# A macaron transformer block on one core: a planner with one clock per engine, and TensorE work beside attention in bursts

## The chip, the core and the metric

The kernel runs on one core of a Trainium2 chip. The core has a matrix engine (TensorE, "PE" in the profile, with its weight loads as "PEld"), three engines for elementwise work (VectorE "DVE", ScalarE "ACT", GpSimd "POOL"), and SyncE ("SP"), which here only issues transfers (DMAs). The engines run their own instruction streams in order and wait for each other by semaphores. The metric is the device time of one execution in microseconds (us), the median of several runs; lower is better.

## The reference

`x` is 2 x 1024 x 512 in float32 (2 sequences of 1024 tokens). The block is

```python
x = x + 0.5 * ffn(layernorm(x))
x = x + attn(layernorm(x))
x = x + 0.5 * ffn(layernorm(x))

def ffn(x):                       # base layer plus two of eight low-rank experts
    probs = softmax(xf @ W_router.T)                      # 8 experts
    topk_p, topk_i = top_k(probs, 2);  topk_p /= topk_p.sum()
    w = sum(one_hot(topk_i) * topk_p)                     # (tokens, 8)
    h = einsum('td,erd->ter', xf, lora_A)                 # rank 16
    return x @ W_base.T + b_base + 2.0 * einsum('ter,eor,te->to', h, lora_B, w)

def bitnet_linear(x, weight, scale_param):
    s = maximum(mean(abs(weight), axis=1), 1e-8)
    y = (x @ sign(weight / s).T) * (s * scale_param)
    return nan_to_num(y, nan=0, posinf=1e6, neginf=-1e6)

def attn(x):                      # q: 32 heads of 16; k, v: 8 heads of 16, each for 4 query heads
    q, k, v = bitnet_linear(x, ...) three times
    attn = softmax(q @ k.T / 4)   # over all 1024 keys, no mask
    return bitnet_linear(attn @ v, o_weight, o_scale)
```

`W_base` is 512 x 512, and all products are to be as exact as float32 makes them: the kernel splits q, k and the inputs of the binarised layers into a high and a low part.

## The kernel before

**Tiles.** Tokens lie in tiles of 128, four tiles to a group, two groups to a sequence: (b, g) = (0,0), (0,1), (1,0), (1,1). `first(b, g)` is what a group does before attention: layer norm (`ln_T`: statistics on DVE, power on POOL, normalised tile on DVE or ACT, transpose on PE, copy on ACT), the first feed-forward (`ffn_tiles`), a second layer norm, and the q, k and v projections (`qkv_part`). `second` is what follows attention: `normalize` (division by the softmax sum), `o_proj`, the second feed-forward. `final` and `last` do the same for the last group, (1,1). `ffn_tiles` has a low-rank and router part (`low`, L359, tiles `phf` or `phs`), the choice of experts on DVE, a transpose (`hwp`, L462), and per tile four base matmuls and one of the experts (L384 and L389, `pbf` or `pbs`; f stands for the first feed-forward, s for the second). `binarize` makes the signs of one weight matrix. `finite` is nan_to_num.

**Attention.** There are 32 units (b, query block of 512, key-value head), in that order of nesting. Each unit has 4 turns. Per unit, 32 `m` tiles (L789: 64 rows, the heads 0 and 2 on the lower and 1 and 3 on the upper half of the rows; 128 queries against 512 keys) give the scores of which DVE takes the row maxima (L797, 128 x 512 each). `m_gather` (L802) and `m_place` join the maxima, transpose them on PE (`mp`, L809), split them on DVE and send them by two DMAs from SP into `mq` (L815). Then 32 `e` tiles (128 keys against 512 queries) are made of two matmuls each: the score (L824) and the subtraction of the maxima (L828, `two_r` times `mq`); ACT takes the exponential (L831) into one of 14 buffers `es`. `a_part` multiplies four exponentials by the values in four column strips, in two halves of 256 queries (L862), into the PSUM bank `av`. `unit_end` copies `av` (L840) and stores it to memory (L843); `place` loads a unit's q and k (L738, L746), `place_v` builds its values.

The turns are software-pipelined: in turn n the kernel issues the `m` tiles of turn n, the `e` tiles of turn n - 5 (LEAD) and the products of turn n - 6. The order within a turn is a string, `TURN` (`LEAD_IN` where there is neither `e` nor `A`). In it `m0(3)` is the m tile 3, `e0(2)` and `e1(2)` the two matmuls of e tile 2, `A0` to `A3` the four products. `F` is a place where one slice of other TensorE work may go, `S` the place of `m_place`, and `V`, `W`, `C`, `D` places where DVE or ACT may take one operation of other work. `m_max` and the exponential are recorded right after their matmul.

**The planner.** All of the program is recorded under a manual schedule: the order in which the kernel records instructions is the order on each engine, and this order comes from a small planner. A piece of work is a generator, a `Strand` with a rank (lower goes first); it yields what it needs next: an engine (P, v, a, g, d for PE, DVE, ACT, POOL and SP's DMAs), the engine its input comes from and since when, and how many PSUM banks it takes. It can also wait for resources (`r`), for conditions (`u`), or for other strands (`j`). `Flow` has one integer clock `t`. A strand may go when `t` has reached the end of its last step plus a delay from the table `LATER` (by pair of engines; one table for attention, one, with shorter delays, for what lies before and after). `offer(kind)` lets one strand record one operation, and then the engine is taken for `LASTS` ticks. `play` goes through the five engines at each tick. A tick stands for 0.115 us (`usec`). During attention a turn is worth `BRIEF` = 50 ticks and each slice given 7 more.

PSUM has eight banks: `ps_a` holds `av`, and the pool `ps` has seven for all else. `stock["fb"]` lets other work hold six before attention and two during it.

**The lead-in** starts with `first(0,0)`, `first(0,1)`, `binarize` for k, q, v and o, and `begin`, which places unit 0 and issues its first 16 m tiles. The loop runs until `begin` is done, plus 3 us, and then `attention` takes over. `first(1,0)`, `first(1,1)`, `second` of three groups and `final` are `chains`, started in attention at given turns, at most three at a time. `last` runs at the end. In batch 0 the writes of q to memory are issued on ACT's queue (high part, L573) and POOL's (low part, L580), other writes of q and k on SP's (L584).

Of the kernel before, what the change touches and what calls it, by code (L numbers as in the profile page):

```python
# [15 lines left out]
P = 128  # L16
# [16 lines left out]
def macaron_kernel(ctx: ExitStack, tc: tile.TileContext, x_in, wbT, b_base, wrT, aT, bT,  # L33
# [68 lines left out]
    for e in range(E):  # L102
# [16 lines left out]
    BRIEF, SLICE = 50, 7  # L119
    LATER = {False: dict(Pv=10, Pa=10, PP=0, vP=36, aP=36, gP=40, va=20, av=16, vg=16, ag=14, gv=30,  # L120
                         ga=30, gg=0, vv=0, aa=0, dv=50, dg=50, da=50, dd=0, gd=32, vd=26, ad=26,
                         xd=50, dP=60),
             True: dict(Pv=11, Pa=11, PP=0, vP=8, aP=8, gP=13, va=8, av=8, vg=8, ag=8, gv=13, ga=13,
                        gg=0, vv=0, aa=0, dv=26, dg=26, da=26, dd=0, gd=13, vd=8, ad=8, xd=26,
                        dP=30)}
    LASTS = dict(P=9, v=6, a=5, g=11, d=5)
    SUM = 11
    APART = dict(P=0, v=5, a=5, g=10, d=5)

    class Strand:  # L130
        def __init__(self, gen, rank):
            self.gen, self.rank, self.done, self.last, self.end = gen, rank, False, "P", 0
            self.kind = None

    class Flow:
        def __init__(self):
            self.t, self.free, self.after, self.strands, self.n = 0, True, False, [], 0
            self.stock = dict(m=3, n=4, t=11, xT=2, xL=2, hT=1, fb=6)
            self.lock = None
            self.busy = dict.fromkeys("Pvagd", 0)  # L140
            self.pool = 0

        def spawn(self, gen, rank):
            self.n += 1
            s = Strand(gen, (rank, self.n))
            self.strands.append(s)
            self.strands.sort(key=lambda s: s.rank)
            self.go(s)
            return s

        def go(self, s):

            if s.kind in LASTS:
                s.last, s.end = s.kind, self.t
            if s.kind == "g":

                self.pool = max(self.pool, self.t) + (s.banks or SUM)
                s.end = self.pool - SUM
            w = next(s.gen, None)
            if w is None:  # L160
                s.done = True
                self.strands.remove(s)
                return
            s.kind, s.arg = w[0], w[1]
            if s.kind in LASTS:
                since = w[2] if len(w) > 2 and w[2] is not None else s.end
                s.banks = w[3] if len(w) > 3 else 0
                s.at = since + LATER[self.free and (s.rank[0] < 6 or self.after)].get(s.arg + s.kind, 0) if s.arg else since

        def settle(self):  # L170

            again = True
            while again:
                again, asked = False, set()
                for s in list(self.strands):
# [6 lines left out]
                    elif (s.kind == "r" and not asked & set(s.arg)  # L182
                          and all(self.stock[k] >= c for k, c in s.arg.items())):
                        for k, c in s.arg.items():
                            self.stock[k] -= c
                    elif s.kind == "u" and s.arg():
                        s.end = self.t
# [7 lines left out]
        def give(self, **kw):  # L195
# [3 lines left out]
        def offer(self, kind):  # L199
            if self.t < self.busy[kind]:  # L200
                return False
            self.settle()
            for s in self.strands:
                if s.kind == kind and s.at <= self.t and (
                        kind != "P" or self.lock in (None, s) and s.banks <= self.stock["fb"]):
                    if kind == "P":
                        self.lock = None
                        self.stock["fb"] -= s.banks
                    self.go(s)
                    self.busy[kind] = (self.pool if kind == "g" else  # L210
                                       self.t + (LASTS if self.free else APART)[kind])
                    self.settle()
                    return True
            return False

        def crowd(self, kind):
            return sum(s.kind == kind and s.at <= self.t for s in self.strands)

        def play(self, until):

            for _ in range(20000):
                if until():
                    return
                for kind in "Pvagd":
                    self.offer(kind)
                self.t += 1
            raise RuntimeError([(s.rank, s.kind, s.arg) for s in self.strands])

    flow = Flow()


    def finite(y, o, n, fast, back):
# [9 lines left out]
        if fast:  # L242
            yield "v", src, t
            nc.vector.tensor_scalar(lo_, y, 0.0, -BIG, ALU.min, ALU.max)
            yield "v", "v"
            nc.vector.tensor_scalar(o, y, 0.0, BIG, ALU.max, ALU.min)
            e, eng = ("v", nc.vector) if fast > 1 else ("g", nc.gpsimd)
            yield e, "v"
            eng.tensor_tensor(o, o, lo_, ALU.add)
            last = e, flow.t if e == "v" else flow.pool - SUM  # L250
            yield "v", ""
            nc.vector.tensor_scalar(m_, y, 0.0, 0.0, ALU.mult, ALU.is_equal)
        else:
            yield "g", src, t, 6
            nc.gpsimd.tensor_scalar(lo_, y, 0.0, -BIG, ALU.min, ALU.max)  # L255
            yield "v", src, t
            nc.vector.tensor_scalar(m_, y, 0.0, 0.0, ALU.mult, ALU.is_equal)
# [832 lines left out]
```

## Time and profile before

| | |
|---|---|
| Runs | 3, median 1113.64 us (1112.82 to 1113.84) |
| Profiled execution | span 1111.0 us, 21684 instructions |
| Busy | PE 1059.5 (95%), weight loads 579.2, DVE 882.0 (79%), ACT 677.4 (61%), POOL 290.0 (26%) |
| Maxima L797 on DVE | 1024, 650.4 us busy, mean 683 ns |
| Exponentials L831 on ACT | 1024, 545.6 us busy, mean 599 ns |
| m tiles L789 on PE | 1024, 357.1 us busy, mean 456 ns |
| e tiles L824 and L828 on PE | 1024 each, 329.6 and 275.7 us busy |
| Products L862 on PE | 4096, 275.1 us busy, mean 386 ns |
| Base matmuls L384 on PE | 128 for each feed-forward, 61.2 and 60.9 us busy |

The profile shows one execution; its own time is the span, 2.6 us below the median of the runs. A line "PE 1059.5 (95%) x8453" gives busy time, share of the span and number of instructions. Matmuls overlap in the pipeline of PE, so the busy time of a line is the time in which at least one of its matmuls was under way, and the mean of one is longer than the distance from start to start. A timeline line has the time of the first instruction, the length up to the end of the last, the engine, the line of the code, what is written and read, the shapes, and how many instructions follow each other. The granted clock of PE is given as a share of full speed.

### The profile page before, as it was taken

To read this page: it belongs to the slowest core of one execution; us is meant where nothing else is said; L and a number is where in the kernel's file an instruction comes from. 1 tells how busy PE (TensorE), PEld (TensorE's weight loads), DVE (VectorE), ACT (ScalarE), POOL (GpSimd) and SP (SyncE) were. 2 spreads that over 40 slices of the span, in tenths; PEclk is the share of its full clock that TensorE was granted. 3 is DMA by queue.
4 is the path that set the end of the run, shared out by engine and by line. 5 is a ranking of instruction groups with operands and counts; after the bars stand their busy time and mean duration, and the time that the engine had idled before them with its cause. 6 is when DMAs were issued, how large, how long until landed. Compare 5 with 4: busy or idle time off the path is not lost.

```text
span 1111.0 us, 21684 instructions
## 1 busy us (share of the span) xinstructions
PE 1059.5 (95%) x8453; PEld 579.2 (52%) x8453; DVE 882.0 (79%) x1698; ACT 677.4 (61%) x1309; POOL 290.0 (26%) x347
## 2 busy tenths in 40 slices
PE   5889679999999999999999999999999999999988
PEld 4546345554455654545655455544554444555554
DVE  5667988878788787798798987887779877797375
ACT  2312237766677566677676787666767765668711
POOL 5232753001030021122434212441110230232432
PEclk9989669999999999999999999999999999999999
DMA  9023463211122023245235232222221322221111
GB/s 286 1 76 104 124 170 98 57 34 38 39 67 63 9 81 91 59 114 164 56 123 161 50 120 59 49 56 61 58 59 50 116 73 67 58 70 34 57 48 47
DMA packets 48798, 87.44 MB, mean 79 GB/s; under 512 B 9768, under 2 KB 12840, under 8 KB 48696
## 3 DMA queue, kind: packets, MB, share of 16 engines
q1 hardware_dynamic: 42552, 74.45, 23.2%
q10 hardware_dynamic: 3872, 7.34, 2.1%
q0 software_dynamic: 2272, 4.27, 1.8%
q8 instruction: 66, 1.08, 0.4%
q14 instruction: 36, 0.29, 0.1%
HBM read 51.19 MB, written 34.32 MB: 77 GB/s over the span
## 4 chain that ended last, share of the span: by engine, by line
PE 77%; DVE 17%; DMA 2%; issue 1%; ACT 1%; POOL 1%; SPq 0%; DVEq 0%; POOLq 0%; ACTq 0%
PE av L862 21%; PE m L789 14%; PE e L824 11%; PE e L828 9%; DVE mn L797 9%; PE pbf L384 5%; PE pbs L384 4%; PE pq L537 2%; PE po L675 2%; PE pbf L389 1%; PE phs L359 1%; PE phf L359 1%; PE pbs L389 1%; DMA arw<-in_wrT 1%; PE pv L554 1%
## 5 line engine op out<-in xcount | busy, mean ns | idle before, releaser
L797 DVE TENSOR_REDUCE mn<-m 128x1 f32<-128x512 f32 x1024 | 650.4, 683 | 140.8 <-PE m L789 112.1
L831 ACT ACTIVATE es<-e 128x512 f32<-128x512 f32 x1024 | 545.6, 599 | 266.0 <-PE e L828 258.9
L789 PE MATMUL m<-k 64*128 64x512 f32 x1024 | 357.1, 456 | 9.4 <-DVE mn L797 4.1
L824 PE MATMUL e<-k 64*128 64x512 f32 x1024 | 329.6, 428 | 4.3 <-DVE mn L797 2.1
L828 PE MATMUL e<-mq,two_r 64*128 64x512 f32 x1024 | 275.7, 399 | 1.7 <-DMA mq<-mT 1.7
L862 PE MATMUL av<-es,vaug 128*32 128x256 f32 x4096 | 275.1, 386 | 0.7 <-ACT avs L840 0.3
L789 PEld LDWEIGHTS m<-k 64*128 64x128 f32 x1024 | 147.7, 187 | 138.3 <-DVE mn L797 82.8
L824 PEld LDWEIGHTS e<-k 64*128 64x128 f32 x1024 | 165.3, 185 | 83.8 <-DVE mn L797 54.1
L862 PEld LDWEIGHTS av<-es,vaug 128*32 128x32 f32 x4096 | 107.7, 109 | 135.0 <-issue 88.7
L828 PEld LDWEIGHTS e<-mq,two_r 64*128 64x128 f32 x1024 | 159.2, 186 | 16.2 <-issue 2.2
L384 PE MATMUL pbf<-wb,xTf 128*128 128x512 f32 x128 | 61.2, 605 | 0.1
L384 PE MATMUL pbs<-wb,xTs 128*128 128x512 f32 x128 | 60.9, 606 | 0.0
L400 POOL TENSOR_TENSOR x<-x,hbf 128x512 f32<-128x512 f32 x8 | 10.3, 1282 | 154.5 <-ACT hbf L397 154.5
L627 POOL TENSOR_TENSOR an<-an,rb 128x512 f32<-128x512 f32 x15 | 19.2, 1282 | 111.7 <-DMA rb<-rd 100.0
L379 POOL TENSOR_TENSOR x<-x,bh 128x512 f32<-128x512 f32 x32 | 41.0, 1308 | 0.9 <-ACT xns L301 0.9
L384 PEld LDWEIGHTS pbs<-wb,xTs 128*128 128x128 f32 x128 | 22.8, 189 | 26.8 <-issue 26.4
L384 PEld LDWEIGHTS pbf<-wb,xTf 128*128 128x128 f32 x128 | 22.7, 190 | 26.7 <-issue 25.0
L576 POOL TENSOR_TENSOR z<-z,y 128x512 fp32r<-128x512 f32 x17 | 22.1, 1300 | 46.4 <-ACT y L570 46.3
L260 POOL TENSOR_TENSOR z<-z,loa 128x512 f32<-128x512 f32 x17 | 21.8, 1281 | 42.5 <-DVE z L258 26.4
L400 POOL TENSOR_TENSOR x<-x,hbs 128x512 f32<-128x512 f32 x8 | 10.3, 1286 | 79.8 <-ACT hbs L397 79.8
L255 POOL TENSOR_SCALAR loa<-y 128x512 f32<-128x512 f32 x17 | 11.7, 687 | 72.0 <-ACT y L542 64.6
L260 POOL TENSOR_TENSOR ro<-ro,loo 128x512 f32<-128x512 f32 x16 | 21.1, 1319 | 32.6 <-DVE ro L258 29.5
(207 smaller groups left out, 1009.6 us busy)
## 6 DMA issues: line engine op xcount, KB each, us to landing
k<-qd SPq DMA_DIRECT2D x32, 512.0 KB
k<-kd SPq DMA_DIRECT2D x62, 256.0 KB
ad<-avs SPq DMA_DIRECT2D x32, 256.0 KB
qd<-y SPq DMA_DIRECT2D x18, 256.0 KB
qd<-z SPq DMA_DIRECT2D x18, 256.0 KB
an<-ad SPq DMA_DIRECT2D x15, 256.0 KB
rb<-rd SPq DMA_DIRECT2D x15, 256.0 KB
x<-in_x SPq DMA_DIRECT2D x14, 256.0 KB
```

The source lines that it names most:

```text
L260: nc.gpsimd.tensor_tensor(o, o, lo_, ALU.add)
L359: nc.tensor.matmul(ph[:, i, 0:ER + E], xT[:, c, t * P:(t + 1) * P], arw[:, c, :], start=(c == 0), stop=(c == KC - 1))
L379: nc.gpsimd.tensor_tensor(xt[:, t, :], xt[:, t, :], bh, ALU.add)
L384: nc.tensor.matmul(pb, xT[:, c, t * P:(t + 1) * P], wb[:, c, :], start=(c == 0), stop=False)
L389: nc.tensor.matmul(pb, hT[0][:, t * P:(t + 1) * P], lb, start=False, stop=True)
L537: nc.tensor.matmul(pq, w_[:, k, :], xs[j][:, k, :], start=(k + j == 0), stop=(k + j == KC))
L789: nc.tensor.matmul(s["m", i], s["q"][rows_of(h), h // 2, qt * P:(qt + 1) * P], s["k"][rows_of(h), kh * 512:(kh + 1) * 512], start=True, st ...
L797: nc.vector.tensor_reduce(s["mn"][:, 2 * (h % 2) + h // 2, qt, kh:kh + 1], s.pop(("m", i)), AX.X, ALU.max, negate=True)
L824: nc.tensor.matmul(t, s["k"][rows_of(h), kt * P:(kt + 1) * P], s["q"][rows_of(h), h // 2, :], start=True, stop=False)
L828: nc.tensor.matmul(t, two_r[rows_of(h), h // 2, :], s["mq"][rows_of(h), :], start=False, stop=True)
L831: nc.scalar.activation(e, s.pop(("e", i)), AF.Exp, scale=HD ** -0.5)
L862: nc.tensor.matmul(s["av"][32 * h:32 * h + 32, cols], s["v"][:, kt, :], s["es"][kt * REP + h][:, cols], start=(kt + half == 0), stop=(kt + ...
```

## The change

The planner is replaced. Instead of one clock, `Flow` has a clock in ns for DVE, ACT, POOL and SP, and for PE a model of when a matmul's weights are loaded, when it starts, and when it ends. Wrappers (`VE`, `AE`, `GE`, `SE`, `TE`) stand in front of the engines; each records the instruction and charges a length for it. `play` always lets the operation go that can start first by these clocks. The PSUM banks are a list of the times at which they come free, and so are the 14 `es` buffers; the maxima and the exponentials are queues of their own (`tiles`), which `other` weighs against the strands.

```diff
-    BRIEF, SLICE = 50, 7
-    LATER = {False: dict(Pv=10, Pa=10, PP=0, vP=36, aP=36, gP=40, va=20, av=16, vg=16, ag=14, gv=30,
...
-    LASTS = dict(P=9, v=6, a=5, g=11, d=5)
...
+    SURE, LAND, OLD, HOLD, AGED, EAGER = 120, 5000, (5500, 3000), 3, 8000, 0
+    DRAIN = dict(v=100, a=110, g=75, P=0, d=0)
+    HEAR = dict(v=35, a=35, g=80, P=55, d=70)
...
+        def charge(self, kind, ns):
+            self.clk[kind] += ns
+            self.t = self.clk[kind] + DRAIN[kind]
...
+        def play(self, until, tensor=None):
+            for _ in range(200000):
+                self.settle()
                 if until():
                     return
...
+                ops = [self.other(k) for k in "vagd"] + [(tensor or self.slices)()]
+                ops = [o for o in ops if o]
+                if not ops:
+                    break
+                o = min(ops, key=lambda o: o[0])
+                self.now = max(self.now, o[0])
+                o[1]()
```

In attention, the order string loses its places for other work and is a new one. `tensor` decides at each step what PE gets next. A burst of other work may begin after a block of two products, when at least three strands wait (`WORTH`), or one has waited for over 15 us (`LATE`), or one is urgent (rank -3 or below); it goes on while strands are ready. Other work may hold three banks (`HOLD`). Elsewhere the next score or product of the string goes. `m_gather` and `m_place` become a strand `maxima` of rank -3, started when the last maximum of the unit has been planned; `place` and `place_v` become strands too.

```diff
-    TURN = ("A0 A1 m0(1) m0(6) m0(3) e0(2) e0(3) e1(2) e1(3) m0(2) F F S C e0(6) m0(7) e1(6) e0(1) "
-            "e0(0) e1(1) e1(0) m0(5) V D A2 A3 C m0(0) e0(5) m0(4) e0(7) e0(4) e1(7) V W D e1(4) "
-            "e1(5)")
-    LEAD_IN = ("m0(0) m0(6) m0(1) V m0(7) F C S V m0(4) m0(2) V F C m0(5) V F C V m0(3) V F C V")
...
+    ORDER = ("m0(0) m0(3) A0 A1 e0(2) m0(1) e1(2) e0(5) e0(0) m0(7) e0(6) e1(5) e1(6) e0(1) e1(0) "
+             "e1(1) m0(5) m0(4) A2 A3 m0(2) e0(3) e0(4) e1(3) m0(6) e0(7) e1(4) e1(7)")
...
+    AHEAD, BLOCK, LATE, WORTH, STARVED = 150, 4, 15000, 3, 500
+    AT_ONCE, BIAS = 1, 700
...
+        def tensor():
+            S, A, F = scores(), products(), flow.slices()
+            if flow.lock and F:
+                return F[0], F[1]
+            now = flow.load
+            waits = [s for s in flow.strands if s.kind == "P" and s.at <= flow.enter("F")]
+            urgent = F and F[2].rank[0] <= -3
+            due = F and F[0] <= flow.enter("F") + 50 and (
+                state["burst"] or len(waits) >= WORTH or any(s.at < now - LATE for s in waits) or urgent)
...
+            if due and (mode == "F" and state["burst"] or mode == "A" and state["block"] % 2 == 0):
+                return go(F)
+            if todo and todo[0][0] == "A":
+                return A and (A[0], product_due)
+            return first(S, None, F)
```

Outside attention: `finite` loses its `fast` variants and records its steps in another order, and `pick` chooses DVE or POOL for two of them and for the low part of q and k by the two clocks (with `BIAS` = 700 ns against DVE once unit 0's keys and queries are there). All writes of q are issued from SP. The ranks of the lead-in's strands change, `begin` no longer waits for the second half of unit 0's keys (`later_keys` loads them), and one chain, `first(1,0)`, starts before attention (`AT_ONCE`). For strands with a rank from 10 to 19 the layer norm is in its ACT form at any time (`calm`), and the base matmuls wait for the experts (`early`); `first(1,0)` has rank 10, `first(1,1)` 11 and `last` 12.

```diff
+    def pick(t, v, g):
+        if flow.free and max(flow.clk["v"], t) + v + (BIAS if (0, 0, 0) in ended and not flow.after else 0) <= max(flow.clk["g"], t) + g:
+            return "v", VE
+        return "g", GE
...
-        calm = not flow.free or flow.after
+        calm = not flow.free or flow.after or 10 <= rank < 20
...
-        bs, ready, early = {}, [], flow.free
+        bs, ready, early = {}, [], flow.free and not 10 <= rank < 20
...
-            own = b == 0 and i < KC and not fast
...
+            e, eng = pick(flow.t, 600, 1220)
+            yield e, "a"
+            lo = o[:, :].bitcast(F32R)
+            eng.tensor_tensor(lo, o, y, ALU.subtract)
+            for j, t in enumerate((y, o)):
                 for c in range(2):
...
+                    yield ("d", e) if j + c == 0 else ("d", "d")
+                    SE.dma_start(dst[:, 2 * c + j if i < KC else 2 * j + c, :, :], t)
...
-        flow.spawn(first(0, 0, (4, 0, 5, 1, 2, 3), (0, 0, 5, 5, 5, 5), {4: 1, 0: 1}, [usec(t) for t in (3, 3.7, 6.6, 7.3)]), 0)
+        flow.spawn(first(0, 0, (4, 0, 5, 1, 2, 3), (0, 0, 5, 6, 6, 6), {4: 1, 0: 1}, [usec(t) for t in (3, 3.7, 6.6, 7.3)]), 0)
...
+        flow.spawn(first(0, 1, (4, 5, 0, 1, 2, 3), (3, 5, 12, 12, 12, 12), {4: 2}, [usec(14 + t) for t in range(TG)]), 3)
...
+        flow.spawn(chain_o(), 8)
         early = flow.spawn(begin(), 5)
-        flow.play(lambda: early.done)
-        t0 = flow.t
-        flow.play(lambda: flow.t > t0 + usec(3))
+        flow.spawn(later_keys(), 2)
+        flow.play(lambda: {(0, 0, KC), (0, 0, 0)} <= ended)
...
-        attention(chains, TU // 2)
+        live = [flow.spawn(chains.pop(0)[1](), 9) for _ in range(AT_ONCE)]
+        flow.play(lambda: early.done)
+        attention(chains, TU // 2, live)
```

What is computed, the matmuls and their shapes, and the number of units, turns and tiles stay as they are.

## The prediction

> **What bounds the kernel now.** I read the page first, then the busy time by stage, then TensorE's instructions in order of time for a few attention turns, and last the chain that ended last, for the tail.
>
> ```profile
> span 1111.0 us, 21684 instructions
> PE 1059.5 (95%) x8453; PEld 579.2 (52%) x8453; DVE 882.0 (79%) x1698; ACT 677.4 (61%) x1309; POOL 290.0 (26%) x347
> 0.00:161.05 161.05, 123.70 (x462) 76.24 (x463) 123.52 (x272) 43.16 (x92) 75.50 (x95) 0.85 0.42 121
> 161.05:1052.70 891.65, 885.25 (x7827) 474.43 (x7826) 721.83 (x1349) 625.45 (x1199) 198.29 (x234) 1.00 0.26 73
> 1052.70:1111.00 58.30, 50.56 (x166) 28.49 (x166) 36.66 (x79) 8.79 (x19) 16.20 (x18) 0.97 0.14 50
> 122.00:161.00 39.00, 26.16 (x58) 13.20 (x58) 37.46 (x63) 11.79 (x20) 26.84 (x31) 0.54 0.53 133
> ```
>
> The three middle lines are the lead-in (up to the first value product, L862), the attention stage and the tail after the last product. Columns: length, then busy time of PE, weight loads, DVE, ACT and POOL, then the granted clock. In the attention stage PE is busy 99% at full clock: it is the bound there. The last line is the end of the lead-in: DVE works 37.5 of 39 us and PE runs at 0.54 clock, so there DVE decides.
>
> A busy PE is not a PE at its peak. One attention turn with other TensorE work in it, and one without:
>
> ```profile
> 296.93 1.07 PE L862 MATMUL av<-es,vaug 128*32 128x256 f32 x16
> 297.93 0.72 PE L789 MATMUL m<-k 64*128 64x512 f32 x3
> ...
> 298.50 0.62 PE L828 MATMUL e<-mq,two_r 64*128 64x512 f32 x2
> 298.74 0.39 PE L789 MATMUL m<-k 64*128 64x512 f32 x1
> 299.06 1.98 PE L384 MATMUL pbf<-wb,xTf 128*128 128x512 f32 x4
> 300.97 0.49 PE L824 MATMUL e<-k 64*128 64x512 f32 x1
> ```
> ```profile
> 644.93 0.73 PE L789 MATMUL m<-k 64*128 64x512 f32 x3
> ...
> 645.74 0.39 PE L789 MATMUL m<-k 64*128 64x512 f32 x1
> 645.98 0.38 PE L824 MATMUL e<-k 64*128 64x512 f32 x1
> ...
> 647.83 1.07 PE L862 MATMUL av<-es,vaug 128*32 128x256 f32 x16
> ...
> 650.95 0.50 PE L789 MATMUL m<-k 64*128 64x512 f32 x2
> ```
>
> From starts to starts: a block of two value products takes 1.00 us. Scores run in pairs, one on each half of the rows, a pair each 0.235 us (298.50 to 298.74). A block of eight scores takes 1.13, that is 0.94 for four pairs and 0.19 for entering. The visit to the base matmul takes 1.91 for four passes at 0.43, again some 0.2 for entering. The second fence: where no other work splits it, the order puts m(2) and e(6) next to each other, both on the same half, and they go alone (645.74, 645.98); the 16 scores then take 2.90 where 8 pairs and one entry would be 2.07. The whole turn is 6.02 us.
>
> **The attention stage, priced.** Counting blocks in the order of the built programs, between the first and the last product: before 256 product blocks, 358 score blocks, 105 visits of other work; after 255, 267 and 51 (22 of these a single transpose of maxima). Scores are 3008 and 3006, other matmuls 561 and 537.
> Before: products 256 x 1.00 = 256; scores 3008 x 0.117 + 358 x 0.19 = 420; other work, each kind at its own start-to-start time (0.43 a pass of the base matmuls, 0.23 a 512-column projection, 0.11 a transpose), 152.6, and 105 entries at 0.16 on average = 16.8. Sum 845.6 of 891.65; the 46 left are waits and scores that went alone. 21 of the 16-score blocks are in it, 0.85 each = 18.
> After: products 256, scores 351.7 + 267 x 0.19 = 402.4, other work 155.5 + 51 x 0.14 = 162.5. Sum 821. **Fewer entries are worth 24.5 us**; these are counted, not guessed.
>
> **The waits in the new turns** are the open part. Each turn still has eight maxima on DVE:
>
> ```profile
> 1003.29 3.68 DVE L797 TENSOR_REDUCE mn<-m 128x1 f32<-128x512 f32 x6
> ```
> Six in 3.68, the last one 0.68 long: 0.60 each in a row, 4.8 a turn. A new turn without other work has blocks of 14 and 10 scores: 2 x 1.00 + 24 x 0.117 + 2 x 0.19 = 5.2 us. It alternates the halves all through, and it spreads the m tiles, two to four between products. Laid out by hand with 0.53 us from a score's start to DVE, 0.46 to ACT, 0.60 and 0.49 a tile, eight maxima end 0.4 us a turn before they must, and no tile waits for one of the seven banks; the products wait about 0.1 us for the fourth exponential. Three costs on top:
> - The subtraction of the maxima. The strand of m_gather and m_place now starts when the last maximum is planned, and in 17 of 32 units only 21 matmuls (10 scores, a product block, two scores: 2.9 us) lie between the transpose and the first L828 of that unit; before it was 38 (5.0 us). At 633.77 the transpose ran, at 635.87 SP issued mq, and at 639.48 it was used, with no wait. So it needs between 2.9 (no wait) and 5.6 us (issue to use in the lead-in, the one place where it is waited for): 0 to 2.7 a unit. With DVE and SP free I take 0.5: 17 x 0.5 = 8.
> - The fourth exponential, 68 turns (four in each of those 17 units) x 0.1, and 32 copies of av (0.59 on ACT) before the next exponential, 0.3 each: 17.
> - Strands whose inputs come later than the planner's clock says, and DVE work that lands between maxima: before, the visits cost 3.7 more than their price; I take 13 for the 29 real bursts.
> Sum 38 in place of 46. Bounds: none (stage 821, 70 less) and, upward, turns at the old pace (the last rival). **Attention stage: 821 + 38 = 859, 32 less.** DVE alone would not hold that up: 722 us of work against 859.
>
> **The lead-in.** The first sequence of x(1,0) up to its first base tile now comes before attention: 46 more matmul instructions there, 14.5 us by the prices above, and 8.5 us more DVE work before the 44th maximum (102.7 to 111.2, each operation at its mean time). In the stretch where DVE decides, though, less is left: the statistics of x(1,0) (5 x 0.87, counting 0.18 for each aggregate) and the reciprocals of s_o (4 x 0.83) move ahead of the first m tile, where DVE was busy only 20.3 of 30 us. From the first m tile to the first product I count 49 us of DVE work, against 71 us that passed before. Against that stands a later q projection: phf of the first two tiles now stands ahead of ptf of the others, and hwpf ahead of pbf, about 3 us. Also the 28 writes of q that ACT and POOL issued now go to SP, 0.6 each, 17 us of SP's time; z must be ready before what is queued behind it, unit 1's keys among them, but these are needed 15 us later. Bounds: 18 less (DVE without a gap) and 9 more (the added DVE work in full). I take **8 less**, nearer to the first, as DVE ran at 96% in the last 39 us.
>
> **The tail.**
>
> ```profile
> 1052.70 3.63 PE pbs L384 x8
> ...
> 1065.13 1.84 PE po L675 x8
> ```
> The base matmuls at 1052 to 1065 belong to the group before; they filled the time in which the last unit is stored, inverted and read back. They now run in the attention stage (their 17 us are in its sum), and the tail does not become shorter, since po waits for the same chain. Worse, PE stands still for 12 us: after a similar pause (60 to 65) the trace shows clock 0.51 up to 71, so the 26 po matmuls that are left (six go before the last piece has landed) cost 0.2 more each for 3 to 7 us: about 2. The condition `not 10 <= rank < 20`, written for ranks 10 and 11, also holds back `last`, rank 12: its base tiles wait for hT and stand behind hwps, so the 3.4 us of pbs that ran during the top-k of the first pair, twice, come afterwards, less 2.9 of transposes and phs that move the other way. **5 more** (0 to 9).
>
> A rule that speaks against the change: the trace has the unmixed turn at 6.02 us with DVE busy 5.45, and the mixed one at 6 to 7 with PE busy throughout. The Trainium skill, "Perfetto Trace Analysis", Optimization Strategy, says that a kernel with stages of different limits may gain by interleaving them. By it the unmixed turns stay at DVE's pace, and the sum would be the last rival's.
>
> **Sum.** 1111.0 - 32 - 8 + 5 = 1076; the median of the runs lies 2.6 above this execution's span, so 1079.
>
> **Rivals.**
> 1. The entries are saved and nothing else: waits stay 46, the lead-in stays, the tail pays 5. 1113.6 - 24.5 + 5 = 1094. For it: new bursts make new waits at their edges. Against: the lone scores at 645.98 go for certain.
> 2. DVE paces the turns (slower). With no other work to fill, PE waits at the m tiles as at 644.93 to 650.95. If all 128 turns take the old 6.02, the stage is 128 x 6.02 + 162 = 933, 41 more, and 1113.6 + 41 - 8 + 5 = 1152 is the end. It decides from 5.72 a turn on, where the sum is the old one. For it: DVE was busy 5.45 of 6.02 there. Against: 0.8 of those 6.02 are the lone scores, and the maxima need 4.8.
> 3. The planner's clocks drift from the chip's, so that bursts stand on PE before their inputs are there: one late strand in each of the 29 bursts by 1.2 us eats all: 1114.
>
> **How the numbers follow.** Forecast 0.62, with its own range 1050 to 1100; rival 1 0.17; rival 3 0.07, split over the three signs; rival 2 0.14. Faster takes the first two and a little of the third, 0.80; within 0.2% (what a measurement of this kernel can tell from no change) 0.03; slower 0.17. The range leaves out what is beyond 1120 of rival 2, and the best ends together (stage 60 less, lead-in 18 less): 1046 to 1120.
>
> **What would show it.** Right: a turn without other work at 5.2 to 5.5, L789 and L824 in unbroken pairs, 50 or so visits; first L862 near 153; PE idle some 12 us after the last L862 and a low clock behind it. Wrong: idle of PE put down to `mn` at L789 in most turns (rival 2), to mq in more than 1 us a unit, or to xT, hT or DMA at the head of bursts (rival 3).

## The result, and the profile after

The changed kernel takes 1123.74 us (median of 4 runs, 1122.37 to 1124.76) against 1113.23 before: 1.0101 of it, with an interval of 1.0086 to 1.0116. It is slower; the forecast was 1079, with a range of 1046 to 1120.

The page of the profile after, and the busy time by stage (length, then PE, weight loads, DVE, ACT, POOL, and the granted clock). In this kernel the wrappers record the instructions, so all DVE operations have line 334, all matmuls 377, transposes 381.

```profile
span 1122.3 us, 21909 instructions
PE 1046.2 (93%) x8453; PEld 631.1 (56%) x8453; DVE 886.9 (79%) x1704; ACT 673.7 (60%) x1313; POOL 278.0 (25%) x327
0.00:178.17 178.17, 139.14 (x536) 87.24 (x536) 135.27 (x309) 52.43 (x112) 74.35 (x91) 0.88 0.39 126
178.17:1059.70 881.53, 870.53 (x7796) 521.13 (x7794) 718.87 (x1316) 613.00 (x1185) 195.21 (x226) 1.00 0.26 72
1059.70:1122.30 62.60, 36.57 (x124) 22.70 (x124) 32.74 (x80) 8.24 (x18) 8.46 (x10) 0.83 0.08 30
111.15:178.17 67.02, 55.92 (x212) 34.66 (x211) 60.89 (x118) 19.16 (x36) 36.70 (x36) 0.82 0.53 173
```

By stage, spans of the two profiled executions:

| | before | after | difference | forecast |
|---|---|---|---|---|
| lead-in, to the first product | 161.05 | 178.17 | +17.1 | -8 |
| attention stage | 891.65 | 881.53 | -10.1 | -32 |
| tail | 58.30 | 62.60 | +4.3 | +5 |

The loss is in the lead-in, and two thirds of the expected gain in the attention stage is missing.

**The lead-in.** TensorE's instructions of the changed kernel in order of time; in brackets the idle time before and what ended it:

```profile
26.50 0.69 PE L381 MATMUL hwpf<-ident,hwf 128*128 128x128 f32 x2 [4.71 <-DVE hwf L334]
26.98 6.22 PE L377 MATMUL pbf<-wb,xTf 128*128 128x512 f32 x8
...
71.67 0.66 PE L381 MATMUL hwpf<-ident,hwf 128*128 128x128 f32 x2 [5.60 <-DVE ksc L334]
72.12 5.83 PE L377 MATMUL pbf<-wb,xTf 128*128 128x512 f32 x8
77.39 0.79 PE L377 MATMUL pq<-ka,sign_k 128*128 128x512 f32 x1
...
111.15 0.73 PE L377 MATMUL m<-k 64*128 64x512 f32 x4
```

Twice TensorE stands at the transpose of the experts' inputs (`hwpf`) while DVE still chooses experts, and the base matmuls behind it wait as well. After each pause eight of them take 6.22 and 5.83 us in place of the 3.60 they take at full clock; the granted clock is 0.56 from 26.5 to 33.0 and 0.57 from 71.6 to 77.4. The kernel before:

```profile
20.49 3.60 PE L384 MATMUL pbf<-wb,xTf 128*128 128x512 f32 x8
...
47.77 0.48 PE L537 MATMUL pq<-ka,sign_k 128*128 128x512 f32 x1
...
65.01 0.66 PE L462 MATMUL hwpf<-ident,hwf 128*128 128x128 f32 x2 [4.63 <-DVE topf L424]
65.32 0.78 PE L537 MATMUL pq<-ka,sign_q 128*128 128x512 f32 x1
...
89.59 0.79 PE L789 MATMUL m<-k 64*128 64x512 f32 x2
```

In the first group its base matmuls stood ahead of the transpose; in the second it stood there too, once, for 4.63 us. The first k projection now comes at 77.4 (before 47.8), the first q projection at 81.4 (65.3), and the first m tile at 111.15 (89.59), 21.6 us later. So the pauses are only part of this: up to the first m tile TensorE is idle for 27.9 us (before 20.7) and busy for 83.2 (68.9). Of the 21.6 us, 7.2 are standing and 14.3 work: 64 more matmul records lie ahead of the first m tile (the k projection of the second group, sums for `binarize` of o, transposes of group (1,0), half of the value projections), most of them from 96.8 on.

**The attention stage.** A turn without other work, TensorE:

```profile
448.60 1.07 PE L377 MATMUL av<-es,vaug 128*32 128x256 f32 x16
449.60 0.49 PE L377 MATMUL m<-k 64*128 64x512 f32 x1
449.60 0.72 PE L377 MATMUL e<-k 64*128 64x512 f32 x2
...
450.95 1.18 PE L377 MATMUL av<-es,vaug 128*32 128x256 f32 x16
452.06 0.50 PE L377 MATMUL e<-k 64*128 64x512 f32 x1
452.06 0.50 PE L377 MATMUL m<-k 64*128 64x512 f32 x1
...
453.90 0.42 PE L377 MATMUL av<-es,vaug 128*32 128x256 f32 x4
```

It takes 5.30 us, and scores start in pairs all through, as forecast. Over the 80 turns without other work the median is 5.39 (6.04 before, 23 turns). But a turn that follows a burst looks like this, TensorE and then DVE:

```profile
487.50 1.07 PE L377 MATMUL av<-es,vaug 128*32 128x256 f32 x16
...
490.89 0.39 PE L377 MATMUL m<-k 64*128 64x512 f32 x1
492.44 0.50 PE L377 MATMUL m<-k 64*128 64x512 f32 x1 [1.16 <-DVE mn L334]
492.87 1.82 PE L377 MATMUL av<-es,vaug 128*32 128x256 f32 x16
...
496.80 0.42 PE L377 MATMUL av<-es,vaug 128*32 128x256 f32 x4
```
```profile
487.06 1.50 DVE L334 TENSOR_SCALAR ro<-yo 128x512 f32<-128x512 f32 x1
...
489.00 1.27 DVE L334 TENSOR_REDUCE mn<-m 128x1 f32<-128x512 f32 x2
490.19 1.62 DVE L334 COPY_PREDICATED ro<-mo,yo 128x512 f32<-128x512 uint8 x1
491.71 2.47 DVE L334 TENSOR_REDUCE mn<-m 128x1 f32<-128x512 f32 x4
494.10 0.68 DVE L334 BATCH_NORM_STATS2 sto<-x 128x6 f32<-128x512 f32 x1
```

It takes 9.30 us. Three o_proj tiles ran in one burst (471.8 to 477.4) and a fourth from 484.2, and their nan_to_num and statistics now stand between the maxima; DVE has hardly a gap, TensorE waits for it. The 1.16 us of standing are not all of it: from 492.44 to 496.06 the granted clock is 0.58, and the product block takes 1.75 us in place of 1.00. Taking each turn's length less the other TensorE work in it, less 5.35, and adding up over all turns, gives 35 us, 28 of it in turns in which DVE is idle for 0.4 us or less. In the visits of other work, 165 us in all from their start to the next instruction of attention, DVE is busy for only 62 us; before it was 157 of 173.

### The profile page after: what moved, and what is told of

Read it like the earlier page. It is cut to its first block, busy times and chain, and to the rows that moved or that the text cites. A ratio compares the mean times of both kernels' runs of the same rounds, so it can differ in the third digit from the quotient of the medians.

```text
span 1122.3 us, 21909 instructions
## 1 busy us (share of the span) xinstructions
PE 1046.2 (93%) x8453; PEld 631.1 (56%) x8453; DVE 886.9 (79%) x1704; ACT 673.7 (60%) x1313; POOL 278.0 (25%) x327
## 5 line engine op out<-in xcount | busy, mean ns | idle before, releaser
L348 ACT ACTIVATE es<-e 128x512 f32<-128x512 f32 x1024 | 537.2, 608 | 148.7 <-PE e L377 146.9
L377 PE MATMUL m<-k 64*128 64x512 f32 x1024 | 343.8, 434 | 15.0 <-DVE mn L334 14.9
L377 PE MATMUL e<-k 64*128 64x512 f32 x1024 | 319.3, 426 | 3.9 <-DVE mn L334 2.7
L377 PE MATMUL av<-es,vaug 128*32 128x256 f32 x4096 | 292.4, 386 | 0.5 <-ACT avs L348 0.2
L377 PEld LDWEIGHTS m<-k 64*128 64x128 f32 x1024 | 158.8, 185 | 97.9 <-DVE mn L334 59.0
L377 PEld LDWEIGHTS e<-k 64*128 64x128 f32 x1024 | 167.5, 185 | 78.8 <-DVE mn L334 47.6
L377 PEld LDWEIGHTS av<-es,vaug 128*32 128x32 f32 x4096 | 132.3, 109 | 112.9 <-issue 73.0
L377 PEld LDWEIGHTS e<-mq,two_r 64*128 64x128 f32 x1024 | 145.1, 185 | 20.0 <-issue 4.3
L377 PE MATMUL pbf<-wb,xTf 128*128 128x512 f32 x128 | 64.6, 654 | 0.1
L362 POOL TENSOR_TENSOR x<-x,bh 128x512 f32<-128x512 f32 x32 | 40.8, 1293 | 15.8 <-DVE w_f L334 10.1
L334 DVE BATCH_NORM_STATS2 stf<-x 128x6 f32<-128x512 f32 x32 | 21.8, 683 | 19.9 <-POOL x L362 16.3
L377 PE MATMUL po<-sign_o,anxT 128*128 128x512 f32 x64 | 27.4, 428 | 10.2 <-ACT anxT L348 10.2
L348 ACT CAST y<-z 128x512 fp32r<-128x512 f32 x20 | 12.7, 633 | 34.2 <-DVE z L334 34.1
```

What stands on the lines that cost most here:

```text
L334: return f(out, *a, **kw)
L348: return f(out, *a, **kw)
L362: return f(out, *a, **kw)
L377: return nc.tensor.matmul(out, lhsT, rhs, **kw)
```

## The experiments

Theory 1 at the start: in the attention stage DVE paces the turns between bursts, since it falls idle in the bursts; in the lead-in TensorE stands behind inputs that the planner's clock believes to be there. The rivals: TensorE's entries and waits pace the turns; the lead-in simply has more work in it. Every edit of the planner's constants makes it plan everything anew, so a stage can change by some microseconds for reasons beside the edit. Only E5 keeps the recorded order as it was. All but E13 and E14 are single executions: E13's six lie between 1102.5 and 1109.3 us, and in the seven traces whose order up to the first m tile is the same (the changed kernel, E1, E2, E4, E5, E6, E9) this tile starts between 109.3 and 111.8.

**E1, less DVE work in attention.** `masked` is `flow.free` as it stands when the strand comes to `finite`.
```diff
-        VE.tensor_scalar(m_, y, 0.0, 0.0, ALU.mult, ALU.is_equal)
+        if masked:
+            VE.tensor_scalar(m_, y, 0.0, 0.0, ALU.mult, ALU.is_equal)
...
-        yield ("v", *last)
-        VE.copy_predicated(o, m_, y)
+        if masked:
+            yield ("v", *last)
+            VE.copy_predicated(o, m_, y)
...
```


> The changed kernel, but nan_to_num leaves out its mask test and its predicated copy where it is planned during attention (26 of each, about 0.33 and 0.60 us from start to start on DVE: 24 us of DVE work less). Theory 1 (DVE paces the turns between the bursts, where it has hardly a gap): the attention stage of 881.5 us gets 12 to 24 us shorter, DVE's idle time outside the bursts stays near 60 us. Theory 2 (TensorE's entries and waits at the edges of the bursts pace it): the stage changes by less than 4 us. Both: lead-in 178 and tail 62.6 us within 1 us.

Span 1110.1 us; lead-in 174.4, stage 873.9, tail 61.8. The stage is 7.6 shorter, between the two theories; the lead-in, 3.8 shorter, was to stay within 1 us. The excess in turns without idle DVE, 28 us in the changed kernel, is 9. A new wait may hide part of the gain:

```profile
307.66 0.76 PE L377 MATMUL e<-mq,two_r 64*128 64x512 f32 x1 [7.32 <-DMA mq<-mT]
```

SP issued mq at 299.43, behind 14 writes of q in the 20 us before, and it could be used 8.2 us later. If the wait could simply be taken off, the stage would be 15 shorter (an estimate). The sign is that of theory 1, its size is not settled by this run.

**E2 and E6, the bursts undone.** E2 ends a visit after two steps; E6 counts the time of other work in a turn and begins no more of it beyond 600 ns. In both one waiting strand is enough. The conditions are the first (`CAP` = 2) and the second (`SHARE` = 600).
```diff
+            if state["n"] >= CAP and (S or A):
+                F = None
...
+            if F and state["ns"] >= SHARE and F[2].rank[0] > -3 and (S or A):
+                F = None
```


> The changed kernel with its bursts undone: a visit of TensorE to other work ends after two steps of the planner, and one waiting strand is enough for a visit. 99 visits of mostly 4, 5 and 8 matmuls in place of 51 with up to 61. Planner, order of the scores and lead-in stay. Theory 1 (in a burst DVE falls idle, and its work is then added between the maxima of the turns that follow): DVE is busy in over 110 us of the visits in place of 62 of 165, and the attention stage falls from 881.5 to 840 to 860 us. Theory 2 (long bursts save entries and cost nothing): the stage grows by 48 entries at 0.35 us, to about 898 us.

> The changed kernel, but other TensorE work may begin in a turn only while less than 600 ns of it lie in that turn, and one waiting strand is enough. By the built order the other work then lies in 95 of the turns, with 87 to 110 visits of 4 to 9 matmuls, like before the change (96 turns), in place of 27 turns and 51 visits. (In the run with visits of two steps it lay in 38 turns, so that run did not spread it.) Theory 1 (DVE's work per turn is nearly constant, so a turn with little other work is paced by DVE, and a turn with much of it leaves DVE idle; what counts is how evenly the other work is spread over turns): the stage falls from 881.5 to 840 to 865 us, and DVE is busy in more than 110 us of the visits. Theory 2 (entries decide): the stage is 895 us or more.

```profile
178.11:1078.34 900.23, 886.61 (x7797) 521.41 (x7796) 711.79 (x1315) 614.85 (x1185) 195.54 (x227) 0.99 0.25 70
```
```profile
175.48:1074.79 899.31, 890.37 (x7797) 518.00 (x7796) 703.39 (x1315) 617.00 (x1185) 194.16 (x227) 1.00 0.25 71
```

The stages of E2 and E6 take 900.2 and 899.3 us. Theory 1 missed both times: DVE was busy in only 71 and 77 us of the visits, though the work lay in 38 and 95 turns. 48 and 59 visits more at 0.35 us an entry make 17 and 21 us, measured 18.7 and 17.8. E2's agreement is in part luck: in its stage the clock is granted at half for 17 us, in E6's and the changed kernel's for 3.4, and this alone costs up to 7 us. So the runs fit a saving by fewer entries in the changed kernel, but, with all else planned anew, don't show its price by itself. Spreading the bursts did not pay in either.

**E5, cheaper maxima, same order.**
```diff
-        VE.tensor_reduce(..., s.pop(("m", i)), AX.X, ALU.max, negate=True)
+        flow.charge("v", 60 + 512 * 1.05)
+        nc.vector.tensor_reduce(..., s.pop(("m", i))[:, 0:256], AX.X, ALU.max, negate=True)
...
-        AE.activation(e, s.pop(("e", i)), AF.Exp, scale=HD ** -0.5)
+        AE.activation(e, s.pop(("e", i)), AF.Exp, scale=HD ** -0.5 / 64)
```


> The changed kernel in the same recorded order, with each row maximum taken over 256 of the 512 keys of its tile and the exponential's scale divided by 64 (so that it can't overflow): the softmax is not the reference's. On DVE each maximum should take about 0.33 instead of 0.60 us from start to start. Theory 1 (DVE paces the turns between the bursts): turns without other work go from 5.3 to 5.4 us to the 5.04 us that the last three turns of the unit sequence have, which have no maxima left, the slow turns after the bursts vanish, and the attention stage falls from 881.5 to 810 to 835 us. Theory 2 (TensorE paces them): the stage stays above 870 us.

```profile
171.62:1029.93 858.31, 852.87 (x7796) 521.48 (x7794) 494.32 (x1315) 612.03 (x1185) 199.84 (x226) 1.00 0.26 74
```

The stage falls by 23.2 us to 858.3, between the two expectations. The turns without other work keep their median (5.38 in place of 5.39), so these are not paced by DVE; the 5.04 us of the last turns belong to turns with few or no m tiles, and are no floor for the others. The excess over 5.35 falls from 35 to 14 us, 2 of it in turns without idle DVE (28 in the changed kernel), and the turn of 9.30 us now takes 6.15. So DVE cost 21 to 23 us. Turn by turn, 23.1 of the 23.2 us come from the 65 turns with more than 0.5 us of DVE work other than maxima, and 0.1 from the other 62. That 858.3 is close to the 859 of the forecast does not confirm its terms (see below).

**E14, the same DVE work, later.** On the kernel of E10 below, other work goes ahead of maxima only after 30 us of waiting.
```diff
-    SURE, LAND, OLD, HOLD, AGED, EAGER = 120, 2500, (5500, 3000), 3, 8000, 0
+    SURE, LAND, OLD, HOLD, AGED, EAGER = 120, 2500, (5500, 3000), 3, 30000, 0
```


> The same kernel, where an operation of other work goes ahead of waiting maxima on DVE only once it has waited for 30 us (8 us before). The sum of DVE's work does not change, only its place. Theory 1a (the turns after a burst are slow because other DVE work stands ahead of the maxima; kept back, it would fill the 0.5 us that DVE has free in each later turn): the attention stage falls from 877.4 by 8 us or more. Theory 1b (it is the amount of work, wherever it stands): less than 3 us either way.

Stage 875.1 against 877.8 in E13 on the same chip: 2.7 shorter, theory 1b's number. So it is rather the amount of work that comes due together than its place ahead of the maxima.

**E9, the upper clip on POOL in attention.**
```diff
-        VE.tensor_scalar(o, y, 0.0, BIG, ALU.max, ALU.min)
+        if flow.free:
+            VE.tensor_scalar(o, y, 0.0, BIG, ALU.max, ALU.min)
+        else:
+            yield "g", src, t
+            GE.tensor_scalar(o, y, 0.0, BIG, ALU.max, ALU.min)
```


> The changed kernel, where nan_to_num's upper clip goes to POOL in place of DVE while it is planned in attention (some 26 operations of 0.33 us alone on DVE, up to 1.4 us where they ran beside POOL). Theory 1 (in the turns after a burst DVE sets the pace, 20 to 30 us in all): the attention stage falls from 881.5 by 5 to 12 us. Theory 2 (the excess of those turns lies elsewhere): by less than 3 us, or the longer chain through POOL makes it longer.

Theory 1 missed: the stage grows to 891.4, which theory 2 allowed for. Three turns after bursts are 9.4 to 10.9 us long, with DVE idle for 2.1 to 2.4 us. DVE and then TensorE in the longest of them:

```profile
494.99 1.77 DVE L334 COPY_PREDICATED ro<-mo,yo 128x512 f32<-128x512 uint8 x1 [2.02 <-POOL ro L362]
496.66 2.46 DVE L334 TENSOR_REDUCE mn<-m 128x1 f32<-128x512 f32 x4
```
```profile
497.39 0.79 PE L377 MATMUL m<-k 64*128 64x512 f32 x1 [2.96 <-DVE mn L334]
498.11 1.93 PE L377 MATMUL av<-es,vaug 128*32 128x256 f32 x16
```

DVE stands at the predicated copy until POOL is done (the clip takes 1.9 us there, 0.42 on DVE in the tail of the same run), the maxima queue behind it, and TensorE stands and then runs slowly: in this stage the clock is granted at half for 27 us, against 3.4 in the changed kernel. That can cost up to 12 us; the stage grew by 9.9.

**E3, the planner's length of small DVE operations.**
```diff
-                flow.charge("v", 60 + n * dict(...).get(name, 1.05))
+                flow.charge("v", max(300, 60 + n * dict(...).get(name, 1.05)))
```


> The changed kernel, where the planner charges every DVE operation with at least 300 ns (it charges 70 to 100 ns for the small ones of the choice of experts, the trace has 0.15 to 0.2 us and up to 1.1 us beside POOL). By this the first base matmuls stand ahead of the transpose of the experts' inputs again, as before the change, and the first k projection ahead of most base matmuls of the second group. Theory 1 (the lead-in lost its time by matmuls that stand on TensorE behind inputs which the planner's clock believes to be there): the first m tile starts at 94 to 102 us in place of 111.2, the first product at 160 to 170 in place of 178.2. Theory 2 (the lead-in is longer because more work lies ahead of it, the first sequence of group (1,0)): the first product within 4 us of 178. The attention stage within 10 us of 881.5 by both.

```profile
20.25 2.12 PE L378 MATMUL phf<-arw,xTf 128*128 128x136 f32 x16 [0.24 <-ACT xTf L349]
22.21 7.03 PE L378 MATMUL pbf<-wb,xTf 128*128 128x512 f32 x16
29.07 0.38 PE L382 MATMUL hwpf<-ident,hwf 128*128 128x128 f32 x2
```

Sixteen base matmuls stand ahead of the transpose again, without a pause and at full clock. The first m tile comes at 101.6 and the first product at 167.5, as theory 1 had it. The stage grew by 8.7 to 890.2, so that the span, 1120.2, hardly changed. About 5 us of this can come from the clock, granted at half for 14 us of the stage; the rest is not explained. Up to the first m tile TensorE is now idle for 17.6 us (27.9 in the changed kernel) and busy for 84.0 (83.2): what E3 takes away is the standing.

**E7, group (1,0) not started before attention,** with E3's edit (`AT_ONCE` = 0).

> The changed kernel with the planner's 300 ns for small DVE operations (which brought the first product from 178.2 to 167.5 us) and with group (1,0) not started before attention. Theory 1 (the rest of the lead-in's loss is the work of group (1,0) ahead of the first tiles): first product at 157 to 163 us. Theory 2 (the rest lies in what is queued ahead of the first m tile, the value projections): first m tile still at 100 us or later, first product at 165 us or later.

First m tile 94.0, first product 168.2: neither expectation as a whole. The m tiles start 7.6 us earlier than in E3, and nothing of it arrives at the first product.

**E4, E10 and E13.** E4 narrows the rank condition; E10 has E3's and E4's edits and a shorter landing time, and E13 is the same kernel again.
```diff
-        calm = not flow.free or flow.after or 10 <= rank < 20
+        calm = not flow.free or flow.after or 10 <= rank < 12
-        bs, ready, early = {}, [], flow.free and not 10 <= rank < 20
+        bs, ready, early = {}, [], flow.free and not 10 <= rank < 12
...
-    SURE, LAND, OLD, HOLD, AGED, EAGER = 120, 5000, (5500, 3000), 3, 8000, 0
+    SURE, LAND, OLD, HOLD, AGED, EAGER = 120, 2500, (5500, 3000), 3, 8000, 0
```


> The changed kernel, with the condition for ranks 10 to 19 narrowed to 10 and 11, so that the strand of the last group, rank 12, no longer falls under it: its base matmuls may run before the experts are chosen and its layer norm has the DVE form. Theory 1 (the condition costs the tail its 3 to 4 us, as the prediction put it): the tail goes from 62.6 to 58 to 60 us. Theory 2 (the tail is longer because TensorE stands still for 12 us and then runs at a low clock): the tail stays at 61.5 us or more. Lead-in and attention stage stay within 1 us by both.

E4: tail 61.1, 1.5 less than the changed kernel, between the theories. The other part is seen in TensorE's order there, of the changed kernel:

```profile
1071.46 0.80 PE L377 MATMUL po<-sign_o,anxT 128*128 128x512 f32 x1 [10.18 <-ACT anxT L348]
...
1074.06 0.63 PE L377 MATMUL po<-sign_o,anxL 128*128 128x512 f32 x1
...
1078.06 0.40 PE L377 MATMUL po<-sign_o,anxL 128*128 128x512 f32 x1
```

TensorE stands for 10.2 us, and then starts a matmul every 0.43 us for 5 us before it is back at 0.23: some 2 us, as forecast. In the other runs with the narrowed condition the tail takes 58.9 to 60.3 us, but 63.7 in E12; in those without it 61.8 to 63.8.

> The changed kernel with the planner's 300 ns for small DVE operations, 2.5 in place of 5 us for the landing of a load (so that the first m tiles are recorded ahead of half of the value projections), and the rank condition narrowed to 10 and 11. Theory 1 (the rest of the lead-in's loss is the order on TensorE ahead of the first m tile): first m tile at 92 to 96 us in place of 101.6 in the run with 300 ns alone, and the first product at 158 to 164. Theory 2 (from the first m tile on DVE decides, whatever the order on TensorE): first m tile at 92 to 96 us as well, but the first product at 165 us or later.

E10: first m tile 92.8, first product 164.7, between theory 1's 164 and theory 2's 165; stage 877.4, tail 60.3; 1104.2 us. Up to the first m tile TensorE is idle for 17.9 us, as in E3, and busy for 74.9, 9.1 less: here it is work that went behind the first m tile.

> The kernel of the run with 300 ns, 2.5 us and the narrowed rank condition once more, timed in rounds against the kernel before: the single run had 1104.2 against 1112.1 us. If that holds: ratio 0.991 to 0.995; if it was chance: 0.998 or more.

```profile
0.00:163.36 163.36, 133.72 (x536) 86.91 (x537) 132.36 (x311) 52.53 (x112) 72.26 (x89) 0.91 0.40 127
163.36:1041.17 877.81, 870.25 (x7796) 517.70 (x7794) 712.41 (x1316) 613.39 (x1185) 195.74 (x227) 1.00 0.26 74
1041.17:1100.70 59.53, 36.14 (x124) 22.69 (x124) 33.51 (x80) 8.54 (x18) 8.78 (x10) 0.81 0.09 31
```

E13: 1103.35 us (median of 6), 0.9934 of the kernel before, interval 0.9913 to 0.9955. With E14's edit it is 1099.96 and 0.9905 (0.988 to 0.993). Both are faster than the kernel before and the changed one; their intervals overlap.

**E11 and E12,** E10's kernel with E9's clip on POOL, E12 with 180 ns in place of 300.

> The run with 300 ns, 2.5 us and the narrowed condition, and the upper clip on POOL in attention as well. If the parts add: lead-in 158 to 164, attention stage 876 to 885 (the 300 ns made it 9 longer, the clip takes 5 to 12), tail 61: 1095 to 1110 in all, against 1111 before. If the planner's new order in attention undoes this: 1112 or more.

> As the run before, with 180 instead of 300 ns for small DVE operations. By the built order the first base matmul stands ahead of the first transpose of the experts' inputs again, as before the change, and the first m tiles ahead of all value projections. If the lead-in goes by the order ahead of the first m tile: first m tile at 92 to 98 us, first product 158 to 166; if by DVE: first product 165 or later.

E11: lead-in 161.0, stage 889.6, tail 60.1, 1112.5 us: with the clip on POOL the gain is gone. E12: first m tile 94.2, but first product 171.8; stage 883.5; 1120.8 us. So 180 ns, which is nearer to the 0.15 to 0.2 us that the small operations take alone, gave the slower kernel.

**E15, nan_to_num on DVE in the lead-in,** E10's kernel with `BIAS` = -100000 in place of 700.

> The same kernel, where nan_to_num and the low parts of q and k stay on DVE in the lead-in as long as the planner chooses (a bias of 100 us towards DVE). In the changed kernel's trace an upper clip takes 0.34 us alone and 1.03 on average where it overlaps work of POOL. Theory 1 (from the first m tile on DVE decides, and a third of its time there comes from this overlap): each operation gets shorter, but DVE gets some 20 operations more (0.33 to 0.60 us each), so that the first product stays within 5 us of 164.7 us, and the mean of the clips and masks there falls below 0.5 us. Theory 2 (POOL's chain decides there): the first product comes 8 us earlier or more.

First m tile 89.1, first product 156.4, which is what theory 2 expected; clips and masks hardly got shorter (over the kernel on average 0.68 us for the clips of q and k, 0.66 with those of v, and 0.51 for the masks; in E10 0.64, 0.72 and 0.51). But with 14 fewer other matmuls of the program (24 records of the trace) ahead of the first product, the last product ends at 1046.3 us, against 1041.2 in E13: work was moved, not saved. What sets the stretch from the first m tile to the first product, 62 to 78 us in all these runs (71.5 before, 67.0 after), stays open. E5, with the same order and cheaper maxima, has the 62.0, but E1 and E9 have 63.3 and 64.6 with the maxima as they were.

**E8, the order string alone, in the kernel before.**
```diff
-    ... m0(2) F F S C e0(6) m0(7) e1(6) e0(1) e0(0) e1(1) e1(0) m0(5) V D ...
+    ... m0(2) F F S C m0(7) e0(6) e0(1) e1(6) e1(1) e0(0) m0(5) e1(0) V D ...
```


> The kernel before with its own planner, where only the order string is changed: the second block of scores in a turn begins on the other half of the rows (m7 e6 e1 ... in place of e6 m7 ...), so that no two scores on the same half stand next to each other where no other work splits them. Theory A (those turns lose 0.8 us to scores that run alone): the 23 turns without other work go from 6.02 to 5.2 to 5.5 us, and the nine with only a transpose likewise, 16 to 25 us less in the attention stage of 891.7. Theory B (DVE paces those turns anyway): less than 5 us.

The turns without other work still have a median of 6.04 us, the stage takes 892.1 (span 1109.6). Theory B's number, though not by DVE alone, which is idle for up to 1.3 us in these turns. The order that put two scores on one half next to each other was not what made them long: with the new order two scores still start alone (644.58, 644.82), and TensorE still pauses within the turn, 0.59 us up to 645.41 where the kernel before paused 0.60 up to 646.81. What sets this pause stays open.

## Why the forecast was wrong

**Fewer entries, 24.5 us: right, as far as the runs tell.** E2 and E6 paid 18.7 and 17.8 us for 48 and 59 visits more, E2 in part through the clock. The visits' own time was 165 us against 162.5.

**A turn of 5.2 to 5.5 us: right** (median 5.39). The reason given for the old 6.02, scores that the order makes go alone, worth 0.8 us, did not hold (E8); it served against the rival on DVE and carried no term of the sum. ("The last rival" in the prediction is its rival 2, DVE.)

**Waits of 38 us in the attention stage: wrong, 60.** The failed term is the 13 us for strands that come late and "DVE work that lands between maxima". E5 leaves 37, so DVE cost some 23 us more than was allowed, the clock after its waits included. The sentence that misled was "DVE alone would not hold that up: 722 us of work against 859". The stage contains 165 us of visits, in which DVE had little to do; outside them it was busy for 657 of 717 us. Rival 2 named the engine, but put the wait into every turn; it came in the turns after bursts.

That the rest, 37, is near the 38 of the sum is luck. The term of 8 for the subtraction of the maxima shows as 0.4 us of waits for mq in the changed kernel's stage. Of the term of 17, waits on the copies of av show 0.2. In their place an unmixed turn takes 5.39 where its blocks add up to 5.2, some 15 us over the 80 such turns. What these 0.2 us a turn are stays open.

**The lead-in, 8 less: wrong, 17 more, and outside the bounds of 18 less and 9 more.** Two steps failed. The first is the q projection "about 3 us" later; it came 16.1 us later, and the first m tile 21.6. Both reasons, `hwpf` ahead of `pbf` and `phf` ahead of `ptf`, were seen in the built order, but priced by their own lengths and not by what they wait for: 4.71 and 5.60 us of standing, with some 6 us at about half the clock after each, where the kernel before stood for 4.63 once, with the slow clock behind it too. And the TensorE work that moved ahead of the first m tile, 14.3 us more busy time, the slow clock in it, had no price there at all. E3 took 9.5 of the 21.6 us back by taking the standing away, E10 18.4 by also moving work behind the tile, both by the planner's lengths alone. The second step is the 49 us of DVE work from there on: at 0.60 a maximum and the shortest time that the trace has of each other operation (up to the start of the next) it is 50.9, so the count was right, but as they ran DVE was busy for 60.9, in a stretch of 67.0. The 10 us more lie in the operations other than maxima. Rival 3, planner's clocks that drift from the chip's, was the right mechanism for the standing, at the wrong place: I priced it in the bursts of attention at 0.07.

**The tail, 5 more: right in the sum,** 4.3. About 2 came from the low clock, as priced. The rank condition cost 1.5 in E4, where the prediction had 3.9 (6.8 less 2.9); the rest is not accounted for.

## What to carry to other kernels

Where an engine's share is read for a stage, take out the stretches in which it can't work before comparing its work with the stage's length: 722 us in 860 looked like room; 657 in 717 had little, and in 98 of the 127 full turns DVE was idle for 0.4 us or less. A built order shows who stands behind whom; the price of a swap is the wait for the late input and the clock after the pause, not only the length of what was put ahead. Here two small numbers in the planner's table cost more than the better order saved: with 300 ns for small operations, 2.5 us for a landing and the narrowed condition, the same planner beat the old kernel by 0.7%. The number that helped was not the measured one, 300 ns against 0.15 to 0.2 us alone, and with 180 the single run E12 was slower than E11. So it seems to work through the order that it gives, and not by being right.

## What was not expected of the hardware

All times of DVE here are from the changed kernel's trace, each operation up to the start of the next. A clip of 128 x 512 for q and k (SBUF to SBUF) took 0.335 us where no POOL operation overlapped it (8 of them) and 1.03 on average, up to 1.49, where one did (12); predicated copies of the same size, for q and k, 0.64 and 0.98 (10 each). The row maxima, read from PSUM, did not change: 0.622 and 0.614. The two 8 KB transfers of mq could be used 8.2 us after issue behind the writes of q in E1, and 5.6 us after issue in the lead-in of the kernel before, where TensorE waited for them both times; at 639.48 in the kernel before, 3.6 us were enough.
